# Four-way packed scores in a fused transformer pair: where the transposes of the first attention stand, and how the first half's finishing is cut

## The chip, the cores and the metric

The kernel runs on one core of one Trainium2 chip. The metric is device time in microseconds, the median of several executions. Profiles are of one execution of the program. TensorE is written PE, VectorE DVE, ScalarE ACT, GpSimd POOL and the DMA queue's engine SP.

## What is computed

Four layers on one sequence of T = 1024 tokens of D = 256 channels in fp32: an attention, a mixture of 8 experts, a gated linear attention, a mixture of 16 experts. Each is wrapped in two normalisations and a residual. Only the first matters here:

```
def _L0_attn_ref(X, ln_w, ln_b, W_in, W_out):
    Xn = (X - mu) * rsqrt(var + LN_EPS) * ln_w + ln_b
    Q, K, V = split(Xn @ W_in, 3)                # 16 heads of 16 channels
    Q, K = _rope(Q), _rope(K)
    probs = softmax(Q @ K.T / sqrt(16))          # every head: 1024 x 1024
    ctx = probs @ V
    return ctx @ W_out + X
...
x = L0_attn_X
x = x + _layernorm(_L0_attn_ref(_layernorm(x), ...))
x = x + _layernorm(_L0_ffn_ref(_layernorm(x), ...))
...
```

## The kernel before

`attention0` (L325) holds the first layer. The 16 heads lie in four groups of four, NG = 4; a head takes a slot of 32 rows (SLOT), so that a group of four fills the 128 rows of the array. The queries are taken in two halves of 512 tokens. That makes eight steps (query half, group), half 0 first.

The softmax is done in two passes over the scores. The generator `largest` (L380) computes for each step all products of queries and keys once, only for their maxima: it has 16 pulls per step, and each pull makes two products of 32 rows by 512 columns (L396), for two heads, and two maximum reductions on VectorE (L401). The negated maximum is put beside the query's channels. `attend` (L423) then computes the scores again, transposed (L443), with that maximum in them, exponentiates on ScalarE (L472) and multiplies with the values (`gather`, L437). It goes over TT = 8 tiles of keys, `st`, and in each over two pairs of heads. One pair is called a half-step here: two scores, two exponentials, and a gather of the tile before. In half-steps of st = 0 and in the first of st = 1 no gather is made. Sixteen half-steps make one attend.

The two passes are woven. `attend` yields between the two scores of a pair; there the outer loop calls `pull(1)`, which makes two products of `largest`, 20 pulls ahead of attend's own half-step from the ninth half-step on. Pair numbers run in opposite directions in the two generators, so the four products of a half-step use the four different strips of 32 rows of the array. The last 20 half-steps have no pull left; there `attend` goes another way (the branch `alone()`, L453), with four of its own scores together, exponentials at L461.

Three kinds of other work are put into the same place, between the first and the second score of a half-step, all by the order in which the generators emit:

- `turned` (L349): four transposes of 128 x 128 (L354) and a copy by ScalarE (L355). It brings keys (`kT`), queries for the first pass (`unsigned`, `qT`) and queries with their maximum (`signed`, `qTm`) into the layout of the products. `largest` calls it at its pulls s = 1, 9, 11, 13 and, at the very end, 15.
- what `beside` yields, in the first steps only: the projection of the later tokens, and `merged` (L245).
- from the fifth attend (n = NG) on, `finished(0)`, the finishing of the first half's 512 tokens: by token (transposes L492, reciprocal and product L497, L498), by channel (transposes L507, copy L509), `projected` (products with w_out L517, sum L524), and then `turn_over` (L191), which normalises, adds the residual, normalises again (`scales`: statistics L180 and L181, power on GpSimd L184, L185), writes `h` (L206) and leaves the transposes of `h` (L216, copy L217) on the list `todo`. One of these pieces is taken per half-step, so that all are made in the fifth attend.

The finishing of the second half goes onto `todo` after the last attend and is made among the experts' products.

PSUM tiles of this stage come from a pool of seven banks (`a_ps`, all under the tag b1), which scores of both passes and every transposed tile share; an eighth holds the gather's sum. A tile framework gives out these tiles, puts in the waits, and may move an instruction that is not ready behind others.

Of the kernel before, what the change touches and what calls it, by code (L numbers as in the profile page):

```python
# [15 lines left out]
P = 128  # L16
# [3 lines left out]
D = 256  # L20
# [29 lines left out]
class Net:  # L50
# [137 lines left out]
    def pair(self, v, tp):  # L188
        return [v[:, 2 * tp + i, :] for i in range(2)]

    def turn_over(self, ps, tts):  # L191

        nc = self.nc
        tp = tts[0] // 2
        xs = self.pair(self.x, tp)
        rs, nb = self.scales(self.pair(self.acc, tp))
        for i, x in enumerate(xs):
            nc.vector.scalar_tensor_tensor(  # L200
                x, self.acc[:, 2 * tp + i, :], rs[:, i : i + 1], x, ALU.mult, ALU.add
            )
        rs2, nb2 = self.scales(xs)
        h = self.row.tile([P, 2, D], F32, tag="h2", name="h")
        for i, x in enumerate(xs):
            nc.scalar.activation(  # L206
                h[:, i, :], x, AF.Identity, scale=rs2[:, i : i + 1], bias=nb2[:, i : i + 1]
            )
        for i, x in enumerate(xs):
            nc.gpsimd.tensor_scalar(x, x, nb[:, i : i + 1], None, ALU.add)  # L210

        def turned(ps):
            pt = ps.tile([P, KC, 2, P], F32, tag="b1", name="pt")
            for i in range(2):
                for k in range(KC):
                    nc.tensor.transpose(pt[:, k, i, :], h[:, i, k * P : (k + 1) * P], self.ident)  # L216
            nc.scalar.copy(  # L217
                self.hT[:, :, 2 * tp * P : (2 * tp + 2) * P], pt.rearrange("p k i t -> p k (i t)")
            )

        self.todo.extend([None, None, turned])

    def catch_up(self, ps, n):

# [100 lines left out]
    def attention0(self):  # L325
# [4 lines left out]
        with ExitStack() as ctx:  # L330
# [49 lines left out]
            def largest(first):  # L380
# [6 lines left out]
                for n, (qh, g) in enumerate(steps):  # L387
                    raw = raws.pop(n)
                    pm = self.small.tile([P, QT, G, 2], F32, tag="pm", bufs=2, name="pm")
                    for s, (kh, tt, pair) in enumerate(order):  # L390
                        if n == 0 and s == len(order) // 2:
                            turned(kT[:, 0, half(1)], 0, 1, 1)
                        scs = [ps.tile([P, HALF], F32, tag="b1", name="sc") for _ in range(2)]
                        for i, sc in enumerate(scs):
                            r = rows(2 * pair + i)
                            nc.tensor.matmul(  # L396
                                sc, raw[r, tt * P : (tt + 1) * P], kT[r, g, half(kh)],
                                start=True, stop=True,
                            )
                        for i, sc in enumerate(scs):  # L400
                            nc.vector.tensor_reduce(  # L401
                                pm[:, tt, 2 * pair + i, kh : kh + 1], sc, AX.X, ALU.max
                            )
                        if s % 2 == 1:
                            next(first, None)
                        if n > 0 and s == 1:
                            signed(n - 1)
                        if n + 1 < len(steps):
                            nqh, ng = steps[n + 1]
                            if nqh == 0 and s in (9, 11):  # L410
                                turned(kT[:, ng, half((s - 9) // 2)], ng, 1, (s - 9) // 2)
                            if s == 13:
                                unsigned(n + 1)
                        if s == len(order) - 1:
                            nc.vector.tensor_reduce(
                                qk[:, qh * QT : (qh + 1) * QT, 0, g * G : (g + 1) * G, DH : DH + 1],
                                pm, AX.X, ALU.max, negate=True,
                            )
                            if n == len(steps) - 1:
                                signed(n)  # L420
                        yield

            def attend(qh, g, alone):  # L423


                qm = ready.pop((qh, g))
# [23 lines left out]
                for st in range(TT):  # L450
                    pe = [pp.tile([P, 2, HALF], F32, tag="pe", name="pe") for _ in range(G // 2)]
                    pairs = list(reversed(range(G // 2)))
                    if alone():  # L453
# [8 lines left out]
                        if before is not None:  # L462
                            gather(st - 1, before, 1, True)
                        before = pe
                        yield
                        yield
                        continue
                    for at, pair in enumerate(pairs):
                        for i in range(2):
# [1 line left out]
                            score(sc, st, 2 * pair + i)  # L471
                            nc.scalar.activation(pe[pair][:, i, :], sc, AF.Exp, scale=scale)  # L472
                            if i == 0:
                                yield
                        if before is not None:
                            gather(st - 1, before, at)
                    before = pe
                gather(TT - 1, before, 1, True)
                nc.scalar.copy(oT[:, g, half(qh)], po)

            def finished(qh):

                tps = range(qh * QT // 2, (qh + 1) * QT // 2)
                cxs = {}

                def by_token(tp, i, ps):
                    if i == 0:
                        cxs[tp] = self.row.tile([P, 2, H, DH], F32, tag="h2", name="cx")
                    tt = 2 * tp + i
                    pt = ps.tile([P, H, SLOT], F32, tag="b1", name="pt")  # L490
                    for g in range(NG):
                        nc.tensor.transpose(  # L492
                            pt[:, g * G : (g + 1) * G, :].rearrange("p h c -> p (h c)"),
                            oT[:, g, tt * P : (tt + 1) * P], self.ident,
                        )
                    rec = self.small.tile([P, H, 1], F32, tag="rec", name="rec")
                    nc.vector.reciprocal(rec, pt[:, :, DH : DH + 1])  # L497
                    nc.vector.tensor_tensor(  # L498
                        cxs[tp][:, i, :, :], pt[:, :, 0:DH], rec.to_broadcast([P, H, DH]), ALU.mult
                    )  # L500

                def by_channel(tp, ps):
                    cx = cxs[tp].rearrange("p i h c -> p i (h c)")
                    pc = ps.tile([P, KC, 2, P], F32, tag="b1", name="pc")
                    for i in range(2):
                        for k in range(KC):
                            nc.tensor.transpose(pc[:, k, i, :], cx[:, i, k * P : (k + 1) * P], self.ident)  # L507
                    cT = self.row.tile([P, KC, 2, P], F32, tag="cT", bufs=2, name="cT")
                    nc.scalar.copy(cT, pc)  # L509
                    cxs[tp] = cT  # L510

                def projected(tp, ps):
                    cT = cxs.pop(tp)
                    po = ps.tile([P, 2, D], F32, tag="b1", name="po")
                    for i in range(2):
                        for k in range(KC):
                            nc.tensor.matmul(  # L517
                                po[:, i, :], cT[:, k, i, :], self.w_out[:, k, :],
                                start=(k == 0), stop=(k == KC - 1),
                            )  # L520

                    for i in range(2):
                        tt = 2 * tp + i
                        nc.vector.scalar_tensor_tensor(  # L524
                            self.acc[:, tt, :], self.x[:, tt, :], self.rs0[:, tt : tt + 1],
                            po[:, i, :], ALU.mult, ALU.add,
                        )
                    self.turn_over(ps, [2 * tp, 2 * tp + 1])

                for tp in tps:  # L530
                    for i in range(2):
                        yield lambda ps, tp=tp, i=i: by_token(tp, i, ps)
                for tp in tps:
                    yield lambda ps, tp=tp: by_channel(tp, ps)
                for tp in tps:
                    yield lambda ps, tp=tp: projected(tp, ps)

            first, rsx = self.normed0((0, 1))
            self.load_first(rsx[:, 0:1])
# [13 lines left out]
                nc.gpsimd.tensor_tensor(self.rs0, ve, self.nhalf, ALU.pow)  # L553
                yield from self.merged(ps)

            left = [2 * TT * len(steps)]
            ahead = largest(beside())

            def pull(n):
                for _ in range(n):  # L560
                    if left[0]:
                        next(ahead)
                        left[0] -= 1

            pull(2 * TT + 2)
            after = iter(())
            for n, (qh, g) in enumerate(steps):
                if n == NG:
                    after = finished(0)
                for i, _ in enumerate(attend(qh, g, lambda: left[0] == 0)):  # L570
                    pull(3 if n == 0 and i == 7 else 1)
                    step = next(after, None)
                    if step is not None:
                        step(ps)
                    else:
                        self.catch_up(ps, 1)
            for step in after:
                step(ps)
            self.catch_up(ps, len(self.todo))
            self.todo.extend(finished(1))  # L580


# [737 lines left out]
```

## Time and profile before

| | |
|---|---|
| median of 3 timed runs | 1323.51 us (1322.59 to 1324.91) |
| profiled execution | 1320.31 us, its span 1318.5 us |
| mean granted TensorE clock | 0.986 |
| busy: PE, DVE, ACT, POOL | 1244.9, 731.6, 497.4, 149.4 us |
| attends of the first attention, from the first gather at 76.5 us to the last copy at 339.0 us | 262.5 us |

In rows of the profile L with a number is a line of the kernel, `sc<-qTm,kT` the tiles written and read, and "32*128 32x512" a product with 32 active rows and 128 active columns and 512 columns streamed. A product in fp32 shows as two matmul records. What stands in brackets or behind the last bar is the idle time of that engine before the instruction and who ended it. The starts are in microseconds from the first instruction; ends of matmuls are modelled.

### The profile page before, as it was taken

What the parts mean: (1) busy time and instruction counts of PE and PEld (TensorE: products, weight loads), DVE (VectorE), ACT (ScalarE), POOL (GpSimd) and SP (SyncE); (2) the same over time, 40 slices, a digit from 0 to 9 for tenths busy, and PEclk for the clock granted to TensorE, in tenths of its full rate; (3) what the DMA queues carried; (4) which work ended last, traced back from release to release, by engine and by line L of the source; (5) the groups of instructions that cost most, each with busy time, mean ns of one, the idle gap of its engine ahead of it and who ended that gap; (6) DMA issues with size and microseconds to landing.
All of it is one profiled execution on the core that took longest, in us unless ns stands there. A gap on an engine that the chain in (4) does not pass through costs nothing. (4 is left out here: it accounts for less than half of the span.)

```text
span 1318.5 us, 15710 instructions
## 1 busy us (share of the span) xinstructions
PE 1244.9 (94%) x6088; PEld 729.0 (55%) x6088; DVE 731.6 (55%) x1657; ACT 497.4 (38%) x911; POOL 149.4 (11%) x137
## 2 busy tenths in 40 slices
PE   5899999999999998889999999999998799999997
PEld 2433333332456565456676767676767456655655
DVE  4675665563243335777586777777775633233334
ACT  3256663566441111454545444445445122011111
POOL 2100000100010002111212121211112400000000
PEclk9999999899999999899999999999999899999999
DMA  6000000000005101200212112130211103723000
GB/s 189 1 1 1 1 1 1 0 1 1 1 1 172 53 12 53 83 33 32 72 33 72 50 56 72 33 103 33 73 32 34 61 1 95 218 80 108 32 25 32
DMA packets 38923, 64.42 MB, mean 49 GB/s; under 512 B 4776, under 2 KB 28552, under 8 KB 38848
## 3 DMA queue, kind: packets, MB, share of 16 engines
q1 hardware_dynamic: 38848, 63.41, 15.2%
q8 instruction: 48, 0.79, 0.3%
q14 instruction: 27, 0.22, 0.1%
HBM read 62.12 MB, written 1.28 MB: 48 GB/s over the span
## 5 line engine op out<-in xcount | busy, mean ns | idle before, releaser
L401 DVE TENSOR_REDUCE pm<-sc 128x1 f32<-128x512 f32 x256 | 163.4, 684 | 94.2 <-PE sc L443 56.5
L443 PE MATMUL sc<-qTm,kT 32*128 32x512 f32 x512 | 170.5, 644 | 2.4 <-DVE pm L401 1.7
L648 DVE TENSOR_TENSOR mid<-sg,pu 128x512 f32<-128x512 f32 (+1 forms) x82 | 56.4, 687 | 200.3 <-PE pu L645 166.7
L472 ACT ACTIVATE pe<-sc 128x512 f32<-128x512 f32 x216 | 119.1, 595 | 87.5 <-PE sc L443 59.3
L647 ACT ACTIVATE sg<-pg 128x512 f32<-128x512 f32 (+1 forms) x82 | 48.9, 596 | 270.2 <-PE pg L645 270.0
L396 PE MATMUL sc<-kT,qT 32*128 32x512 f32 x512 | 140.1, 643 | 1.7 <-ACT qT L355 1.1
L969 ACT ACTIVATE sn<-pt,shift,rs 128x128 f32<-128x128 f32 x256 | 93.6, 470 | 106.9 <-DVE shift L965 106.8
L929 PE MATMUL px<-hT,w_l1a 128*128 128x512 f32 x256 | 124.1, 597 | 4.1 <-issue 3.5
L921 DVE SCALAR_TENSOR_TENSOR y<-px,cp,y 128x1023 f32<-128x1023 f32 (+5 forms) x102 | 123.2, 1211 | 2.5 <-ACT y L915 2.5
L184 POOL TENSOR_TENSOR rs<-ve,nhalf 128x2 f32<-128x2 f32 (+1 forms) x29 | 20.8, 717 | 702.6 <-DVE ve L183 698.1
L645 PE MATMUL pg<-hT,w_l1f 128*128 128x512 f32 (+1 forms) x200 | 96.0, 603 | 0.7 <-ACT hT L217 0.7
L671 DVE TENSOR_TENSOR acc<-acc,po 128x512 f32<-128x512 f32 (+1 forms) x61 | 41.1, 674 | 99.7 <-PE po L663 99.7
L645 PE MATMUL pu<-hT,w_l1f 128*128 128x512 f32 (+1 forms) x200 | 94.6, 595 | 0.0
L663 PE MATMUL po<-w_l1f,mid 128*128 128x256 f32 (+1 forms) x400 | 87.5, 379 | 0.0
L443 PEld LDWEIGHTS sc<-qTm,kT 32*128 32x128 f32 x512 | 52.5, 185 | 63.2 <-issue 42.0
L964 POOL TENSOR_TENSOR rs<-ve,nhalf 128x8 f32<-128x8 f32 x32 | 52.4, 1638 | 299.5 <-DVE ve L963 244.7
L437 PE MATMUL po<-pe,va 128*32 128x256 f32 (+1 forms) x832 | 83.3, 444 | 1.9 <-ACT pe L461 1.2
L663 PEld LDWEIGHTS po<-w_l1f,mid 128*128 128x128 f32 (+1 forms) x400 | 76.0, 190 | 13.4 <-issue 3.3
L1063 PE MATMUL pg<-hT,w_l1a 128*128 128x512 f32 x128 | 61.9, 609 | 6.5 <-DVE og L1145 4.8
L645 PEld LDWEIGHTS pu<-hT,w_l1f 128*128 128x128 f32 (+1 forms) x200 | 38.2, 191 | 48.9 <-issue 48.7
L437 PEld LDWEIGHTS po<-pe,va 128*32 128x32 f32 x832 | 18.3, 108 | 84.6 <-issue 63.7
L645 PEld LDWEIGHTS pg<-hT,w_l1f 128*128 128x128 f32 (+1 forms) x200 | 37.9, 192 | 44.7 <-issue 43.3
(196 smaller groups left out, 1936.1 us busy)
## 6 DMA issues: line engine op xcount, KB each, us to landing
spread<-rows SPq DMA_DIRECT2D x32, 512.0 KB, 4.5
w<-w SPq DMA_DIRECT2D x16, 512.0 KB, 5.0
w_l1f<-in_e_gT SPq DMA_DIRECT2D x4, 640.0 KB, 4.0
w_l1f<-in_e_uT SPq DMA_DIRECT2D x4, 640.0 KB, 5.3
w_l1f<-in_e_dT SPq DMA_DIRECT2D x4, 640.0 KB, 7.2
w_l0f<-in_e_wg SPq DMA_DIRECT2D x4, 512.0 KB, 3.7
w_l0f<-in_e_wu SPq DMA_DIRECT2D x4, 512.0 KB, 5.8
w_l0f<-in_e_wd SPq DMA_DIRECT2D x4, 512.0 KB, 6.7
```

What stands on the lines that cost most here:

```text
L396: nc.tensor.matmul(sc, raw[r, tt * P : (tt + 1) * P], kT[r, g, half(kh)], start=True, stop=True,)
L401: nc.vector.tensor_reduce(pm[:, tt, 2 * pair + i, kh : kh + 1], sc, AX.X, ALU.max)
L437: nc.tensor.matmul(po[rows(j), c], va[:, st, g * G + j, :], pe[j // 2][:, j % 2, c], start=(st == 0), stop=(st == TT - 1 and quarter == 1),)
L443: nc.tensor.matmul(sc, kT[rows(j), g, st * P : (st + 1) * P], qm[rows(j), :], start=True, stop=True,)
L472: nc.scalar.activation(pe[pair][:, i, :], sc, AF.Exp, scale=scale)
L645: nc.tensor.matmul(p, w(k), self.hT[:, k, c], start=(k == 0), stop=(k == KC - 1))
L648: nc.vector.tensor_tensor(mid, sg, pu, ALU.mult)
L663: nc.tensor.matmul(po[:, i, :], left[:, at * P : (at + 1) * P], right, start=(n == 0), stop=(n == len(pieces) - 1),)
L921: nc.vector.scalar_tensor_tensor(y[:, at:hi], px[:, at - j : hi - j], column(cw + 4 * h + 3 - j), y[:, at:hi], ALU.mult, ALU.add,)
L929: nc.tensor.matmul(px[:, c], w[:, k, hh * DK : (hh + 1) * DK], self.hT[:, k, c], start=(k == 0), stop=(k == KC - 1),)
L969: nc.scalar.activation(sn[:, n, :], pts[n // 4][:, n % 4, :], AF.Identity, scale=rs[:, n : n + 1], bias=shift[:, n : n + 1],)
L1063: nc.tensor.matmul(pg, wg[:, k, hh * DK : (hh + 1) * DK], self.hT[:, k, c], start=(k == 0), stop=(k == KC - 1),)
```

## The change

It has two parts. First, what `largest` turns is no longer emitted inside a pull: the pull returns it as a function (`then`), and the outer loop calls it when `attend` has emitted its second score, the exponentials and the gather of the half-step. The pulls ahead of the first attend are 20 where they were 18, there each `then` is called at once, and the half-step that had three pulls (n = 0, i = 7) has one.

Second, the finishing of the first half is a generator of its own, `finished_slowly`, with a copy of `turn_over` that yields between its pieces. It is advanced once at the end of every half-step, behind the gather and behind `then`, and yields twice after each piece; so a piece comes every second half-step, and the whole takes 62 of the 64 half-steps of the last four attends. Its projection takes one token tile at a time, with a PSUM tile of its own. `finished(1)` does what it did. The diff, cut to its core:

```
+    def turn_over_slowly(self, ps, tp, acc):
...
+        mv = small("mv", 2)
+        for i in range(2):
+            acc(i)
+            yield
+            stats(mv, i, accs[i])
+            yield
+        rs, nb = scale(mv)
+        yield
+        mv = small("mv", 2)
+        for i, x in enumerate(xs):
+            nc.vector.scalar_tensor_tensor(x, accs[i], rs[:, i : i + 1], x, ALU.mult, ALU.add)
+            yield
+            stats(mv, i, x)
+            yield
+        rs2, nb2 = scale(mv)
+        h = self.row.tile([P, 2, D], F32, tag="h2", name="h")
+        for i, x in enumerate(xs):
+            nc.scalar.activation(
+                h[:, i, :], x, AF.Identity, scale=rs2[:, i : i + 1], bias=nb2[:, i : i + 1]
+            )
+            yield
+        for i, x in enumerate(xs):
+            nc.gpsimd.tensor_scalar(x, x, nb[:, i : i + 1], None, ALU.add)
+        self.turn(ps, h, tp)
+        yield
...
                         if s % 2 == 1:
                             next(first, None)
+                        then = None
                         if n > 0 and s == 1:
-                            signed(n - 1)
+                            then = lambda n=n: signed(n - 1)
                         if n + 1 < len(steps):
                             nqh, ng = steps[n + 1]
                             if nqh == 0 and s in (9, 11):
-                                turned(kT[:, ng, half((s - 9) // 2)], ng, 1, (s - 9) // 2)
+                                then = lambda ng=ng, kh=(s - 9) // 2: turned(kT[:, ng, half(kh)], ng, 1, kh)
                             if s == 13:
-                                unsigned(n + 1)
+                                then = lambda n=n: unsigned(n + 1)
...
                             if n == len(steps) - 1:
-                                signed(n)
-                        yield
+                                then = lambda n=n: signed(n)
+                        yield then
...
                             if i == 0:
-                                yield
+                                yield True
                         if before is not None:
                             gather(st - 1, before, at)
+                        yield False
...
+            def finished_slowly():
+
+                yield
+                yield
+                for tp in range(QT // 2):
+                    cx = self.row.tile([P, 2, H, DH], F32, tag="h2", name="cx")
+                    for i in range(2):
+                        tt = 2 * tp + i
+                        by_token(tt, cx[:, i, :, :], ps)
+                        yield
+                        yield
+                    cT = by_channel(cx, ps)
+                    yield
+                    yield
+
+                    def acc(i):
+                        po = ps.tile([P, D], F32, tag="b1", name="po")
+                        projected(2 * tp + i, cT[:, :, i, :], po)
+
+                    for _ in self.turn_over_slowly(ps, tp, acc):
+                        yield
+                        yield
...
-            pull(2 * TT + 2)
+            while pulled < 2 * TT + 4:
+                then = pull()
+                if then:
+                    then()
             after = iter(())
             for n, (qh, g) in enumerate(steps):
                 if n == NG:
-                    after = finished(0)
-                for i, _ in enumerate(attend(qh, g, lambda: left[0] == 0)):
-                    pull(3 if n == 0 and i == 7 else 1)
-                    step = next(after, None)
-                    if step is not None:
-                        step(ps)
-                    else:
-                        self.catch_up(ps, 1)
-            for step in after:
-                step(ps)
-            self.catch_up(ps, len(self.todo))
+                    after = finished_slowly()
+                then = None
+                for inside in attend(qh, g, lambda: pulled == count):
+                    if inside:
+                        then = pull()
+                        continue
+                    if then:
+                        then()
+                        then = None
+                    next(after, None)
+            for _ in after:
+                pass
```

## The prediction

> **What bounds the kernel now.** I read the page first, then a table of windows cut at the eight calls of `attend` (ends at 138.17, 169.58, 201.00, 256.54, 288.02), then the timeline of TensorE inside one of them, then all engines around 201 to 256.
>
> ```profile
> L401 DVE TENSOR_REDUCE pm<-sc 128x1 f32<-128x512 f32 x256 | 163.4, 684 | 94.2 <-PE sc L443 56.5
> L443 PE MATMUL sc<-qTm,kT 32*128 32x512 f32 x512 | 170.5, 644 | 2.4 <-DVE pm L401 1.7
> L396 PE MATMUL sc<-kT,qT 32*128 32x512 f32 x512 | 140.1, 643 | 1.7 <-ACT qT L355 1.1
> ```
>
> ```profile
> 103.90:138.17 34.27, 34.27 (x258) 11.96 (x257) 20.62 (x34) 20.70 (x38) 0.00 (x0) 1.00 0.00 1
> 169.58:201.00 31.42, 31.42 (x249) 10.97 (x248) 20.62 (x34) 19.31 (x36) 0.00 (x0) 1.00 0.01 1
> 201.00:256.54 55.54, 53.25 (x297) 19.60 (x296) 30.77 (x74) 23.64 (x44) 6.47 (x8) 0.91 0.00 1
> 256.54:288.02 31.48, 31.48 (x249) 10.96 (x249) 20.67 (x34) 19.37 (x36) 0.00 (x0) 1.00 0.01 1
> 317.50:336.80 19.30, 18.80 (x128) 4.74 (x128) 0.00 (x0) 16.94 (x34) 0.00 (x0) 1.00 0.00 1
> ```
>
> The columns of a window are its length, busy PE, PEld, DVE, ACT, POOL, the granted clock and the DMA share. In every attend TensorE has no idle time, VectorE and ScalarE are busy two thirds of it: TensorE's order sets the time. 31.42 holds two turns (`turned`), 34.27 four, so **one turn costs (34.27-31.42)/2 = 1.43 us** and an attend without turns 28.57. 55.54 holds two turns and the whole finishing of the first half, so **the finishing costs 55.54-31.48 = 24.06 us**. In the last row, where the first pass has run out, TensorE (97%) and ScalarE (88%) are both nearly full and VectorE idle.
>
> ```profile
> 149.87 0.69 PE L443 MATMUL sc<-qTm,kT 32*128 32x512 f32 x1
> 149.88 0.70 PE L396 MATMUL sc<-kT,qT 32*128 32x512 f32 x2
> 150.94 0.64 PE L437 MATMUL po<-pe,va 128*32 128x256 f32 x8
> 151.51 0.69 PE L443 MATMUL sc<-qTm,kT 32*128 32x512 f32 x1
> ...
> 155.00 0.69 PE L443 MATMUL sc<-qTm,kT 32*128 32x512 f32 x1
> 156.06 0.66 PE L354 MATMUL pt<-ident,qk 128*128 128x128 f32 x4
> 156.65 1.12 PE L443 MATMUL sc<-qTm,kT 32*128 32x512 f32 x2
> 157.70 0.64 PE L437 MATMUL po<-pe,va 128*32 128x256 f32 x8
> 158.27 0.69 PE L443 MATMUL sc<-qTm,kT 32*128 32x512 f32 x1
> ```
>
> Start, duration, line. A plain half-step: four products (each two passes) lie in four different 32-row strips and run side by side, 149.87 to 150.94 = 1.07 us for all; the gather takes 0.57; the step is 1.64 (others 1.85, mean 1.75). A half-step with a turn: three products 1.06, transposes 0.59, then the fourth product **alone** from 156.65 to 157.70, again 1.05, gather 0.57: 3.27. The fourth product is paid twice because the transposes stand before it.
>
> **The turns.** Behind the gather a turn costs its own transposes, 0.59, or less where the step was one of 1.85. Saved per turn: 1.43-0.55 = 0.9 (bounds 0.5 and 1.05). Turns inside half-steps: 4 in attend 1 (0 is the first), 2 each in 2, 3, 4 and 5: 12 x 0.9 = 10.8 us. ScalarE's copy of a turn (0.59) follows its two exponentials (1.09), 1.68 in a half-step that now lasts 2.2, so it hides. The last turn (attend 6) waits at 311.12 for the final maximum; from 308.34 to 314.61 two steps take 6.27 where 1.64+2.16+0.59 = 4.4 would do: 1.8 saved. In attend 0 two turns save 1.8; the half-step with three pulls (5.06 us, two turns) becomes two ordinary ones of 2.3, against 5.06+1.75 now, 2.1 saved; but the two pulls put ahead of the attends fall where VectorE is full (2 x 1.29 = 2.6 lost). They fill TensorE's 0.67 us wait for the copy at 69.53: together +1.8. **Turns: 14.4 us.**
>
> [...]
>
> **The finishing.** It leaves the quartets too, and is spread as 30 pieces over every second half-step of attends 4 to 7: 21 while the first pass still runs, 9 in the last stretch. Pieces stand two half-steps (3.5 us) apart, so transposes and projections find their inputs ready. Cost then, from rows of 201 to 256:
> - TensorE, always on the path: transposes of 4 tokens' contexts, 2 by channel, 1 turn, 7 x 0.59 = 4.1; projections (1.92 us for two tokens at 221.80) 4 x 0.96 = 3.8. Sum 8.0; the second turn lies in the last stretch, below.
> - VectorE: per token 0.67 (reciprocal 0.25, product 0.42), sum 0.43, statistics 0.5 twice, update 0.43; per pair two `scale` of 1.2. All on 0.45 us slack per half-step (1.75-1.29), 0.9 per piece; a `scale` of 1.2 makes the next reductions 0.8 late and seven PSUM banks hold that. Not hidden in the first four half-steps of an attend, which have no gather and where VectorE is full (eight reductions in 4.99 us): one `scale` and one update, 1.6, and 0.3 for three context pieces. Sum 1.9.
> - ScalarE: in attend 5 the first `h` waits for the `scale` before it, with the next exponentials behind it in the queue and the fourth product behind those: 0.7 (bounds 0 and 1.8).
> - The last stretch: `h` twice 0.55 and the hT copy 0.59 on a full ScalarE, transposes 0.5 on a full TensorE beside them: 1.6. Everything of VectorE there is free.
> - GpSimd: four powers (0.71) and four adds (0.93 each) move later in its queue, which was busy 6.47 of 55 us, and nobody waits for the adds in attention. SP issues no DMA in any moved step.
>
> ```profile
> 226.61 0.16 DVE L185 SCALAR_TENSOR_TENSOR nb<-mv,rs 128x2 f32<-128x2 f32 x1 [0.82 <-POOL rs L184]
> 236.22 1.12 PE L443 MATMUL sc<-qTm,kT 32*128 32x512 f32 x2 [1.69 <-DVE pm L401]
> 236.00:244.00 8.00, 7.78 (x22) 2.66 (x22) 3.65 (x9) 3.62 (x7) 2.53 (x3) 0.60 0.00 0
> 244.00:252.00 8.00, 8.00 (x55) 2.59 (x54) 3.59 (x7) 3.63 (x7) 0.00 (x0) 0.76 0.00 0
> ```
>
> Sum 8.0+1.9+0.7+1.6 = 12.2, so **24.06-12.2 = 11.9 saved**. Part of the 24 is the clock: after VectorE's burst (it waits 0.82 for GpSimd, TensorE then waits 1.69 for VectorE) the granted clock is 0.60 and 0.76, worth 8 x 0.40 + 8 x 0.24 = 5.1 us. [...] 103.90 to 138.17 has four turns and a clock of 1.00. I let the dip go with the stalls; if it comes elsewhere the sum is 5.1 less.
>
> **Sum.** 14.4+11.9 = 26.3. The profiled execution took 1320.3 (span 1318.5), which gives 1294.0; the median of the timed runs, 1323.5, lies 3.2 above it, so I predict 1297. What follows attention (experts) reads hT of the first half, now written two rounds of keys (some 4 us) before attention ends; nothing is expected to wait there (bound 2 us).
>
> **Rivals.**
> - The order is not what the code says (10%). The framework may move an instruction: at 309.40 the gather stands ahead of transposes that the code emits first. If turns slip back into the quartets, only the finishing gains: 1323.5-11.9 = 1312. Against: every other turn of before lies where the code puts it.
> - The finishing stays dear (12%): its pieces hold the queues one by one, or the clock dips all the same; half of its gain and some of the turns' go: about 1308.
> - Better than the sum (8%): inserted groups give ScalarE time, 1.85 steps become 1.64, attention meets no stall: 1287.
> - Slower (5%): PSUM. A step now opens a fifth tile in seven banks and holds it into the next step, whose fourth product must then wait and run alone, 1.05 us. With 12 finishing groups and 17 turns that is 29 x 1.05 = 30.5, more than the 26.3 gained: 1327.7. It decides from 25 split quartets on. For it: steps of 1.85 show that the fourth product already starts late at times (waiting for an exponential). Against: after 2.2 us the previous step's exponentials and first maxima have ended, which leaves four banks.
>
> **Numbers.** Main case 65%: 1290 to 1304. With the costs' bounds (turns 10 to 18, finishing saving 6 to 16) and the neighbours, 8 in 10 lies in 1288 to 1310. Runs of this kernel spread over 0.17%, so about 0.2% (2.6 us) can be told from no change; faster 0.93, slower 0.05, and 0.02 for the dear finishing at its worst, which ends near no change.
>
> **What would show it.** In the after profile: no L396 or L443 product alone between transposes and a gather; attends 2 and 3 near 29.7 us, attend 1 near 30.8; clock 1.00 through attends 4 and 5, which take about 34 and 33; no 1.69 us wait of scores on `pm`. Wrong if attends 2 and 3 stay at 31.4 (turns not moved or a lone product remains), if half-steps after a turn show lone fourth products, or if the last stretch grows by over 4 us.

## The result, and the profile after

The changed kernel took 1309.08 us (median of four executions, 1308.1 to 1309.54) where the kernel before took 1324.21 (1322.59 to 1326.6): a ratio of 0.9883 [0.9866, 0.99], or 15.1 us. Its profiled execution took 1309.17 (span 1307.4). Measured a second time, in five rounds beside other kernels (after_again below), the same program took 1301.4 (ratio 0.9829 [0.9783, 0.9874], span of its profile 1298.9). Whether both measurements used the same chip is not on record. The two profiles of the one program differ by 8.5 us: 5.2 of these lie before the end of attend 0, 0.9 in attends 4 to 7 and 2.4 behind attention. So its gain is known only as 15 to 22 us.

Cut at the end of each attend (the copy of its sum), in us from the profiles:

| | to the end of attend 0 | attends 1, 2, 3 | attends 4, 5, 6, 7 | what follows | span |
|---|---|---|---|---|---|
| before | 106.62 | 34.26 31.42 31.42 | 55.60 31.42 28.91 19.36 | 979.5 | 1318.5 |
| after, first | 110.30 | 30.92 29.75 29.74 | 38.14 31.27 35.05 19.95 | 982.3 | 1307.4 |
| after, second | 105.11 | 30.92 29.75 29.75 | 37.28 30.88 35.37 19.95 | 979.9 | 1298.9 |

Summed up against the forecast:

| us saved | forecast | first | second |
|---|---|---|---|
| attends 1 to 3 (8 turns) | 8 x 0.9 = 7.2 | 6.7 | 6.7 |
| attends 4 to 7 (4 turns, the last turn, the finishing) | 3.6 + 1.8 + 11.9 = 17.3 | 10.9 | 11.8 |
| to the end of attend 0 | 1.8 | -3.7 | 1.5 |
| what follows | 0 | -2.8 | -0.4 |
| sum | 26.3 | 11.1 | 19.6 |

"What follows" takes between 977.6 and 983.6 us in the profiles of the other changed kernels below, whose work there is the same. So the 2.8 us of the first column lie within what differs from one execution to the next.

The costliest groups of the page of the changed kernel, and its windows at the calls of attend (1, 3, 4, 5, and the last stretch; columns as in the prediction):

```profile
L449 DVE TENSOR_REDUCE pm<-sc 128x1 f32<-128x512 f32 x256 | 163.0, 685 | 81.6 <-PE sc L493 49.4
L493 PE MATMUL sc<-qTm,kT 32*128 32x512 f32 x512 | 152.9, 643 | 2.3 <-ACT pe L522 1.6
L444 PE MATMUL sc<-kT,qT 32*128 32x512 f32 x512 | 139.5, 670 | 1.7 <-ACT qT L403 1.1
```

```profile
107.58:138.49 30.91, 30.91 (x257) 11.64 (x256) 20.62 (x34) 20.26 (x38) 0.00 (x0) 1.00 0.01 1
168.24:197.98 29.74, 29.74 (x249) 10.80 (x248) 20.61 (x34) 19.09 (x36) 0.00 (x0) 1.00 0.01 1
197.98:235.40 37.42, 35.68 (x269) 12.67 (x268) 27.40 (x55) 20.95 (x39) 3.26 (x4) 0.98 0.00 1
235.40:267.19 31.79, 31.79 (x253) 11.75 (x253) 19.33 (x31) 19.19 (x35) 0.00 (x0) 0.92 0.00 1
303.00:322.90 19.90, 19.21 (x132) 5.05 (x132) 0.00 (x0) 17.43 (x35) 0.00 (x0) 1.00 0.00 1
```

The scores of attend (L493) are the same 512 records with nearly the same mean (643 ns for 644), but cover 152.9 us where they covered 170.5: fewer of them run with nobody beside them. Attends 1 and 3 lose 3.35 and 1.68 with VectorE's and ScalarE's work unchanged. In the third row the forecast fails to come: TensorE is idle for 37.42 - 35.68 = 1.74 us, and the row after it has a clock of 0.92.

What a turn looks like now, in TensorE's timeline (start, duration, line):

```profile
156.60 0.64 PE L487 MATMUL po<-pe,va 128*32 128x256 f32 x8
157.18 0.66 PE L402 MATMUL pt<-ident,qk 128*128 128x128 f32 x4
157.76 0.69 PE L493 MATMUL sc<-qTm,kT 32*128 32x512 f32 x1
157.77 0.70 PE L444 MATMUL sc<-kT,qT 32*128 32x512 f32 x2
...
158.83 0.64 PE L487 MATMUL po<-pe,va 128*32 128x256 f32 x8
```

From gather to gather 2.23 us, where it was 3.27: the transposes stand alone (0.58), and all four products follow together in 1.07. No lone product is left here.

What went wrong in attend 4 stands in its timeline with all engines; in brackets is the idle time before, and who ended it:

```profile
227.92 0.16 DVE L208 SCALAR_TENSOR_TENSOR nb<-mv,rs 128x2 f32<-128x2 f32 x1 [0.82 <-POOL rs L207]
228.00 0.48 DVE L221 SCALAR_TENSOR_TENSOR x<-acc,rs,x 128x256 f32<-128x256 f32 x1
...
230.00 0.45 DVE L221 SCALAR_TENSOR_TENSOR x<-acc,rs,x 128x256 f32<-128x256 f32 x1
...
232.15 0.16 DVE L208 SCALAR_TENSOR_TENSOR nb<-mv,rs 128x2 f32<-128x2 f32 x1 [0.81 <-POOL rs L207]
232.23 2.48 DVE L449 TENSOR_REDUCE pm<-sc 128x1 f32<-128x512 f32 x4
232.35 0.60 ACT L228 ACTIVATE h<-x,nb,rs 128x256 f32<-128x256 f32 x1 [3.81 <-DVE nb L208]
...
233.48 1.99 PE L493 MATMUL sc<-qTm,kT 32*128 32x512 f32 x2 [1.60 <-ACT pe L522]
```

The code spreads the first `nb`, the two updates of x, the second `nb` and `h` over some ten half-steps, about 18 us. On the chip they lie within 4.5. Twice VectorE waits 0.8 for GpSimd with reductions ready behind, then it owes four of them in a row (2.48). ScalarE, with `h` at the head of its queue, does nothing for 3.81, its exponential comes late, and the fourth product runs alone after a wait of 1.60. In the kernel before, TensorE waited 1.69 at this place for a maximum; here it waits for an exponential, and behind both stands a burst on VectorE. The same happens to the second pair in attend 6, where the last turn then waits 2.15 for its maximum:

```profile
296.21 0.66 PE L402 MATMUL pt<-ident,qk 128*128 128x128 f32 x4 [2.15 <-DVE qk L464]
```

VectorE's own timeline shows the order. In the change (first three lines) `ve`, the first step of `scale`, stands right behind the statistics of the second sum, and `nb` is next. In pinned, an experiment below with the same instructions, four reductions stand between the statistics and `ve`, four behind `nb`, and then comes the update of x, as the code emits them:

```profile
226.25 0.43 DVE L201 BATCH_NORM_STATS2 st<-acc 128x6 f32<-128x256 f32 x1
226.71 0.18 DVE L202 BATCH_NORM_AGGREGATE mv<-st 128x2 f32<-128x6 f32 x1
226.93 0.17 DVE L206 TENSOR_SCALAR ve<-mv 128x2 f32<-128x2 f32 x1
```

```profile
224.38 0.42 DVE L201 BATCH_NORM_STATS2 st<-acc 128x6 f32<-128x256 f32 x1
224.83 0.18 DVE L202 BATCH_NORM_AGGREGATE mv<-st 128x2 f32<-128x6 f32 x1
224.93 1.25 DVE L449 TENSOR_REDUCE pm<-sc 128x1 f32<-128x512 f32 x2
228.09 1.29 DVE L449 TENSOR_REDUCE pm<-sc 128x1 f32<-128x512 f32 x2 [1.91 <-PE sc L493]
229.30 0.16 DVE L206 TENSOR_SCALAR ve<-mv 128x2 f32<-128x2 f32 x1
230.28 0.16 DVE L208 SCALAR_TENSOR_TENSOR nb<-mv,rs 128x2 f32<-128x2 f32 x1 [0.82 <-POOL rs L207]
230.36 2.48 DVE L449 TENSOR_REDUCE pm<-sc 128x1 f32<-128x512 f32 x4
232.75 0.47 DVE L221 SCALAR_TENSOR_TENSOR x<-acc,rs,x 128x256 f32<-128x256 f32 x1
```

The framework has pulled the normalisation of the pair forward to its second sum. One wait of 0.82 with four reductions behind it stands in pinned too, and TensorE then waits only 0.24 (at 231.10). So a single wait of this kind costs little; what stops the products seems to be two of them in one burst, with `h` in front of the exponentials.

### The profile page after: what moved, and what is told of

It reads as the page before. It is cut to its first block, busy times and chain, and to the rows that moved or that the text cites. A ratio compares the mean times of both kernels' runs of the same rounds, so it can differ in the third digit from the quotient of the medians.

```text
span 1307.4 us, 15704 instructions
## 1 busy us (share of the span) xinstructions
PE 1230.2 (94%) x6088; PEld 727.1 (56%) x6088; DVE 732.5 (56%) x1657; ACT 495.6 (38%) x911; POOL 149.1 (11%) x137
## 3 DMA queue, kind: packets, MB, share of 16 engines
q1 hardware_dynamic: 38848, 63.41, 15.1%
## 5 line engine op out<-in xcount | busy, mean ns | idle before, releaser
L493 PE MATMUL sc<-qTm,kT 32*128 32x512 f32 x512 | 152.9, 643 | 2.3 <-ACT pe L522 1.6
L493 PEld LDWEIGHTS sc<-qTm,kT 32*128 32x128 f32 x512 | 50.8, 184 | 55.8 <-issue 32.3
L184 POOL TENSOR_TENSOR rs<-ve,nhalf 128x2 f32<-128x2 f32 (+1 forms) x25 | 17.5, 701 | 472.7 <-DVE ve L183 468.2
```

The lines of the kernel that those rows point to most:

```text
L493: nc.tensor.matmul(sc, kT[rows(j), g, st * P : (st + 1) * P], qm[rows(j), :], start=True, stop=True,)
```

## The experiments

Each kernel was timed in five rounds beside the kernel before on the same chip; the first four shared one chip, the next four another, the last two a third. The medians of before were 1323.6, 1323.73 and 1322.54. In all of them "behind" means behind the gather.

**turns_only**: the turns as in the change; the finishing in large pieces among the products, as before but for one order (see burst_behind); the pulls of before.

```
-            while pulled < 2 * TT + 4:
+            while pulled < 2 * TT + 2:
...
-                    after = finished_slowly()
+                    after = finished(0)
...
                     if inside:
-                        then = pull()
+                        thens = [pull() for _ in range(3 if n == 0 and i == 7 else 1)]
...
+                        finish()
                         continue
```

> The changed placement of the turns alone: the finishing stands among the products as before, and the first pass keeps its old pulls (18 ahead, three in one half-step). Theory (the turns bring most of the gain, the finishing little, because its VectorE chain is still made in one burst): attends 1, 2 and 3 as in the changed kernel (30.9, 29.7, 29.7 us), attend 4 about 53.8, in all 12 to 14 us below before. Rival (the gain is shared about evenly, as predicted, and something at the start ate part of it): the same 12 to 14, but then the changed kernel's further gain must show in attend 4 to 7 and its loss at the start. Against both: if under 8 us, the placement of the turns is not what moved attends 1 to 3.

1314.44 (1311.37 to 1316.96), 0.9927 [0.9903, 0.995]. Attends 1 to 7: 30.92, 29.75, 29.75, 55.88, 29.74, 28.34, 19.37. Attends 1, 2 and 3 give their turns exactly as in the change, and attend 5 gives its two. Attend 4 gives nothing (55.60 before), where 1.8 was expected. In the kernel before, one of its two turns stood in the half-step of the 1.69 wait, and the other (251.04) beside the transposes of `h`, which leave the fourth product alone with or without the turn. The kernel also has a new wait of 1.38 there, for the reason given under burst_behind, so what the two turns are worth in attend 4 is not shown by it. In all this half alone brings about 9, not the 12 to 14 expected.

**finish_only**: the finishing as in the change; the turns among the products, the pulls of before.

```
-                            then = lambda n=n: signed(n - 1)
+                            signed(n - 1)
...
-                        then = pull()
+                        for _ in range(3 if n == 0 and i == 7 else 1):
+                            pull()
```

> The small pieces of the finishing alone, over four attends behind the gather; the turns stand among the products as before, and the first pass keeps its old pulls. Theory: attends 1 to 3 as before (34.3, 31.4, 31.4 us), attend 4 about 39, attends 5 to 7 about 9 us longer than before, in all 4 to 7 us below before. Rival (the prediction's own sum): 11.9 us below before.

1316.88 (1308.39 to 1324.89), 0.9947 [0.9926, 0.9969]. Attends 4 to 7 take 38.34, 32.53, 36.13, 19.95, together 8.3 less than before; attends 1 to 3 are those of before. With turns_only (2.0 less in attends 4 to 7) that is 10.3 of the 10.9 of the change: the parts add up within 0.6.

**burst_behind**: the turns as in the change; the finishing in its large pieces of before, one per half-step, but behind.

```
-                    after = finished_slowly()
+                    after = finished(0)
...
-                    next(after, None)
+                    step = next(after, None)
+                    if step is not None:
+                        step(ps)
+                    else:
+                        self.catch_up(ps, 1)
```

> The changed kernel, but the first half's finishing in its old eight large pieces, one per half-step in attend 4, all behind the gather. Theory (what counts is that the pieces leave the quartets of products; the small pieces do not stay spread anyway): attend 4 takes about 41 us, attends 5 to 7 lose what the spread pieces cost them (about 7 us less than in the changed kernel), so within 3 us of the changed kernel. Rival (spreading is what helps): attend 4 stays near 50 us and the kernel is 6 us or more above the changed one.

1302.87 (1302.11 to 1309.93), 0.9851 [0.9826, 0.9877]. Attends 4 to 7: 46.71, 29.75, 28.06, 19.37, in sum 123.89; the change's are 124.41 and 123.48. Attend 4 was dearer than expected, but leaving the quartets alone brings the finishing all that the change gets from it. The spreading, as the framework carries it out, brought nothing beyond that. In the timeline the old stall is still there, as in the change (second line):

```profile
216.84 2.08 PE L578 MATMUL po<-w_out,cT 128*128 128x256 f32 x4 [1.26 <-DVE acc L582]
226.20 1.20 PE L493 MATMUL sc<-qTm,kT 32*128 32x512 f32 x2 [1.66 <-DVE pm L449]
```

The first line is a wait that the kernel before does not have. The changed code's `finished` emits each token's sum right behind that token's products (`projected`), where before the products of both tokens came first; both use one PSUM tile, and the second token's products wait for the first one's sum. So the large pieces are not quite those of before, and `finished(1)` too has this new order. In "what follows" no cost of it can be seen.

**pinned**: the change, with each piece tied in the issue order: nothing of it on VectorE may go ahead of the last reduction emitted, nothing on ScalarE ahead of the last exponential. No instruction is added or left out.

```
-                            nc.vector.tensor_reduce(
+                            self.red = nc.vector.tensor_reduce(
...
-                            nc.scalar.activation(pe[pair][:, i, :], sc, AF.Exp, scale=scale)
+                            self.exp = nc.scalar.activation(pe[pair][:, i, :], sc, AF.Exp, scale=scale)
...
-                    next(after, None)
+                    with self.tc.issue_after(self.red.ins), self.tc.issue_after(self.exp.ins):
+                        next(after, None)
```

> The changed kernel with the issue order held: each small piece's VectorE instructions stand behind the last reductions emitted before them, its ScalarE instructions behind the last exponential, so that the normalisation is really spread. Theory (the framework pulled the VectorE chain forward into one burst, and that cost attend 4 about 4 us and attend 6 about 3): attend 4 near 33 us, no wait of scores of over 1 us on maxima or exponentials there, clock 1.00 in attend 5; 5 to 8 us below the changed kernel. Rival (VectorE and ScalarE work cannot hide in this stretch, however it is spread): within 2 us of the changed kernel, the waits being many and small.

1295.5 (1295.08 to 1297.98), 0.9788 [0.9767, 0.9808]. Attends 4 to 7: 32.78, 31.97, 31.74, 20.31, in sum 116.80, 7.6 less than the change. Its windows over attends 4 and 5 and the last stretch:

```profile
194.20:224.83 30.63, 30.63 (x253) 11.59 (x253) 22.30 (x41) 18.58 (x35) 0.00 (x0) 1.00 0.01 1
224.83:256.65 31.82, 31.50 (x253) 10.75 (x252) 22.43 (x44) 20.62 (x38) 3.26 (x4) 1.00 0.00 1
289.00:309.50 20.50, 19.66 (x133) 5.28 (x134) 0.00 (x0) 18.33 (x38) 1.85 (x2) 1.00 0.00 1
```

TensorE has no gap in attend 4 and 0.32 in attend 5, the clock is 1.00 in both, and VectorE's work is level (22.30 and 22.43) where the change had 27.40 and 19.33. This is the finishing as the prediction had it. In the whole, the interval of pinned lies clear of the change's first one and overlaps that of its second (after_again); the attends tell the two kernels apart, the second total does not.

**after_again**: the changed kernel once more.

> The changed kernel once more, on the chip of this call. Theory (about 6 us of its time in the first profile were a half-speed clock from 53 to 70 us that comes by chance, since kernels with the same instructions up to there had none): runs of two kinds, some near 1302 to 1303 with a mean clock near 0.985, some near 1308 to 1309 with 0.978 to 0.982. Rival (the dip belongs to the changed kernel): all runs within 1 us of 1309.

1301.4 (1299.44 to 1310.56). Its six executions are 1299.44, 1299.46, 1300.71, 1302.09, 1302.12 and 1310.56, with mean clocks of 0.989, 0.989, 0.987, 0.987, 0.985 and 0.976: within this measurement time follows the clock, (1310.56 - 1299.45)/13 = 0.9 us for each 0.001. The four of the first measurement have 0.978 to 0.984. That accounts for the larger part of the distance and not for all of it: 1308.1 at 0.984 is some 4 us longer than the relation gives, and this rest is open.

**old_pulls**: the change with the pulls of before, 18 ahead and three in half-step 7 of attend 0, all their turns behind.

```
-            while pulled < 2 * TT + 4:
+            while pulled < 2 * TT + 2:
...
-                        then = pull()
+                        thens = [pull() for _ in range(3 if n == 0 and i == 7 else 1)]
```

> The changed kernel with the old pulls: 18 ahead of the first attend, three in its eighth half-step, whose turns all stand behind the gather. Theory (the new pull schedule gained about 2 us, by the end of attend 0: 104.5 in profiles without an early clock dip, 106.6 before): end of attend 0 at 105.4, as in the kernel with only the turns moved, less its share of an early dip; 0 to 2 us slower than the changed kernel. Rival (the two pulls ahead cost what they save): no slower, or faster by up to 1 us.

1302.02 (1300.34 to 1310.63), 0.9838 [0.9796, 0.988], like after_again. The new schedule of pulls is worth nothing that can be seen in the whole. The first product of attend 0 shows why, here in old_pulls and in after_again, neither of which has a half-clock stretch between the start-up and it:

```profile
67.59 0.69 PE L493 MATMUL sc<-qTm,kT 32*128 32x512 f32 x1 [0.68 <-ACT qTm L403]
70.20 0.69 PE L493 MATMUL sc<-qTm,kT 32*128 32x512 f32 x1
```

From there attend 0 takes 35.06 (67.59 to 102.65) with the old pulls and 34.91 with the new ones. Of the latter 1.7 are a half-clock stretch of 3.4 at 76; in the first profile of the change, which has none in attend 0, it takes 32.97. So the schedule takes some 2 us out of attend 0 and puts 2.6 ahead of it. Attend 0 itself takes 37.09 in the kernel before, so its turns save the other 2.03.

**pin_dve**: pinned, but only VectorE's part tied (`self.red`), ScalarE's left free.

```
-                    with self.tc.issue_after(self.red.ins), self.tc.issue_after(self.exp.ins):
+                    with self.tc.issue_after(self.red.ins):
```

> As the kernel with the order held, but only VectorE's instructions are held, ScalarE's not. Theory (VectorE's burst made the loss; ScalarE's h follows by data): within 1 us of the kernel with both held (1295.5), attend 4 near 32.8 us. Rival (the exponentials queued behind h made the loss): 2 us or more slower than 1295.5, attends 5 and 6 longer by as much.

1301.57 (1295.98 to 1310.38), 0.9822 [0.9777, 0.9868]. Attends 4 to 7: 32.78, 32.45, 33.97, 19.95. Attend 4 is whole with VectorE tied alone. Attend 6 is 2.2 longer than in pinned; its timeline says why:

```profile
288.79 0.60 ACT L228 ACTIVATE h<-x,nb,rs 128x256 f32<-128x256 f32 x1 [1.33 <-DVE nb L208]
...
289.93 2.03 PE L487 MATMUL po<-pe,va 128*32 128x512 f32 x8 [1.50 <-ACT pe L511]
```

Where the first pass has run out no reduction comes any more that could hold the pieces back, `h` goes ahead of the exponentials, and the gather waits for them. So both queues have to be held: VectorE for the first pair, ScalarE for the last. The median lies 6 us above the 1295.5 that was expected, with runs from 1296 to 1310. The total cannot tell this kernel from the change or from pinned (the intervals overlap); the attends can.

**pinned_vec**: pinned, and the rotation of the last two token tiles on VectorE in place of GpSimd.

```
-                    self.project0(tt, xn, ps, qk, va, nc.vector if tt < 6 else nc.gpsimd)
+                    self.project0(tt, xn, ps, qk, va, nc.vector)
```

> The kernel with the order held, and the rotation of the last two token tiles on VectorE where GpSimd did it. Theory (the early clock dip follows TensorE's idle 1.6 and 0.7 us at 52 to 55 us, which end with GpSimd's rotation): that idle time goes, 1 to 2 us gained before attend 0, and no dip between 50 and 70 in any run, so runs within 2 us of each other near 1293.5. Rival (VectorE is full in this stretch and its reductions get late): 1 us slower or more than 1295.5, idle time on reductions in its place.

**pinned_vec2**: the same kernel again.

> The kernel with the order held and the rotation on VectorE once more, beside the one with h later on the same chip: near 1293.5 us, attends 4 to 7 as in its first profile (32.8, 32.0, 31.7, 20.3 us); runs above 1296 have a lower mean clock, by 0.001 for every 1.1 us or so.

1293.54 (1291.31 to 1299.49), 0.9766 [0.9727, 0.9804], and 1290.17 (1290.12 to 1294.37), 0.9764 [0.9747, 0.9782]. Attend 0 ends at 103.26 and 101.51, the difference a dip of 3.4 us. The wait at the end of the projections shrinks from 1.59 in the kernel before to

```profile
52.61 0.33 PE L402 MATMUL pt<-ident,qk 128*128 128x128 f32 x1 [0.60 <-POOL qk L371]
```

and the clock is 1.00 from 50 to 70 us in the profile of pinned_vec, where the first profile of the change had a dip (a stretch of half clock) of 17.1 us. With the longer wait the clock from 50 to 60 was 0.63 in the change, 0.66 in turns_only and 0.66 in finish_only, but 1.00 in before, burst_behind and pinned; so few do not show that the shorter wait prevents the dip. Other dips still come, and the runs of pinned_vec lie 8 us apart where 2 were expected. In time it is about 1 us in the profile and no difference from pinned that the intervals can tell.

**h_later**: pinned_vec, with a yield moved: `h` comes a piece after the `scale` that it needs, not in the same piece.

```
             nc.vector.scalar_tensor_tensor(x, accs[i], rs[:, i : i + 1], x, ALU.mult, ALU.add)
-            yield
+            if i == 1:
+                yield
             stats(mv, i, x)
...
         rs2, nb2 = scale(mv)
+        yield
         h = self.row.tile([P, 2, D], F32, tag="h2", name="h")
```

> The kernel with the order held and the rotation on VectorE, and h one piece later than the scale it needs (the first update and the statistics behind it share a piece in return). Theory (in attend 5 h waited 1.26 us for nb, the exponentials behind it came late, and the fourth product of one half-step ran alone, 2.83 us for 1.75): that half-step becomes ordinary, attend 5 near 30.9 us for 31.97, the run 1 us below the kernel with h at once. Rival (h costs its own place in ScalarE's queue): no change in attend 5.

1293.14 (1290.75 to 1294.52), 0.9777 [0.9762, 0.9793]. It is the one stall that pinned still had in attend 5. There (first two lines, pinned) ScalarE stands still for 1.26 and the step takes 2.83; with the yield (third line, h_later) `h` waits for nothing, and the step takes 1.75:

```profile
248.37 0.60 ACT L228 ACTIVATE h<-x,nb,rs 128x256 f32<-128x256 f32 x1 [1.26 <-DVE nb L208]
249.51 1.12 PE L493 MATMUL sc<-qTm,kT 32*128 32x512 f32 x2
```

```profile
247.71 0.60 ACT L230 ACTIVATE h<-x,nb,rs 128x256 f32<-128x256 f32 x1
```

Attend 5 falls from 31.97 to 30.98. This 1.0 us is clear in the attend and lost in the whole: on the same chip pinned_vec2 took 1290.17, and the ranges of the two overlap.

## Why the prediction came out as it did

**The bound** was right where it was used: TensorE's order sets the time of attends 1 to 3 within 0.01 us in every kernel with the turns behind. "In every attend TensorE has no idle time" is too much; the prediction's own row of attend 4 has 55.54 - 53.25 = 2.29.

**The turns**: right. Each saves (34.26 - 30.92)/4 = 0.84 for 0.9. The forecast had taken 0.55 for the transposes; they cost 0.58. The lone product carries it, 1.05 us in the prediction's rows: attends 1 to 3, where none is left, saved 6.7. Attend 5 saves its two in turns_only (1.68), attend 6 only 0.57 there and 0.85 in burst_behind, of 1.8: the final maximum still has to be waited for (0.85 us in both).

**The finishing**: the step that failed is "is spread as 30 pieces over every second half-step". It was costed at 12.2 and took (124.41 - 106.93) = 17.5 in the first profile and 16.5 in the second, where 106.93 is what attends 4 to 7 take without any finishing (29.75 + 29.75 + 28.06 + 19.37, from burst_behind and turns_only). Attend 4 is taken here to be like attend 5 without it. In each of the two profiles some 3.4 of this are the clock: 6.8 us at half speed. The costs in the sum were enough for pieces that stay where the code puts them: pinned, with the same instructions and no half-clock stretch, took 116.80 - 106.93 = 9.9, so the 12.2 was 2.3 too high. The prediction named the framework's moving of instructions as a rival, but for the turns only; they stayed. What it moved was VectorE's small instructions, which no one needed early. Why it thought VectorE free for them was not looked into.

**ScalarE**: "in attend 5 the first `h` waits for the `scale` before it" was right as a mechanism, and pinned shows it: 0.7 expected, 1.0 measured by h_later. In the change it sits in attend 4 and is 3.81 long.

**The last stretch**: 1.6 expected, 0.6 in the change (19.95 against 19.36), part of whose work had been pulled into attend 6, and 0.9 in pinned.

**The pulls**: right, step by step. The turns of attend 0 saved 2.03 for 1.8; the half-step with three pulls saved some 2 for 2.1; the two pulls ahead cost 2.6 as forecast, with the 0.67 wait for the copy gone. The prediction's terms make 2.0, not 1.8. In it the schedule comes to next to nothing, and so it does in old_pulls; the 2 us were an expectation of that run alone.

**The clock**: "I let the dip go with the stalls" holds in pinned (1.00 in attends 4 and 5) and not in the change, whose stalls stayed. And the first stretch brought a dip that no step of the forecast moved. That the row with four turns had a clock of 1.00 says little: four turns are 4 x 0.59 = 2.4 of 34 us, too few to show what transposes do to the clock.

**The signs** that it named: attends 1 to 3 came as said, and no turn in them left a product alone. Attends 4 and 5 took 38.14 and 31.27 for 34 and 33, at clocks of 0.98 and 0.92 for 1.00. Scores no longer waited 1.69 on `pm` but 1.60 on `pe`.

**Rivals.** "The finishing stays dear" gave 1308 by pieces that hold the queues and a clock that dips all the same. The first measurement, 1309.08, reads as if it were this case whole. By the table it is so in part: 6.4 of the 15.2 us missing in that profile lie in attends 4 to 7, 5.5 in the first stretch and 2.8 behind attention. In the second the 6.4 are 5.5, hardly more than 1 us is missing elsewhere, and 1301.4 lies in the main case's 1290 to 1304, where 1309.08 lies outside it and just inside the wider range. "Slower" by PSUM did not come: attends 1 to 3 have no lone fourth product. "Better than the sum" did not come for the change; pinned_vec2 reached 1290.17 by an edit that was not part of it.

A part of the agreement is luck: the burst and the clock loss, which were not forecast, were in part made up for by costs that were put 2.3 too high.

**What stays open**: whether the change is worth 15 or 22 us in a given run. 5.2 of the 8.5 us between its two profiles lie before the end of attend 0, where the first had 17.1 us at half clock and the second 3.4; what sets such stretches off is not shown.

## What to carry to other kernels

Where four small products share the array, put everything else between groups and none of it inside; the four transposes of a turn inside cost a whole product's time again (1.05 us). When work is cut fine to lie under another engine's slack, look at each engine's queue in the order as built, because a scheduler may gather it into one burst again; tie the pieces to the work that they are to follow, on every queue where somebody waits. A gain of under 1% of a kernel whose clock moves is told by the stretch that it changes, with the clock beside it, and only then by the total.

## What the runs showed of the hardware

The granted clock fell to 0.50 for stretches of 3.4, 6.8 and 10.2 us in the profile of before and of 3.4, 6.8, 10.2 and 17.1 us in the first profile of the change, multiples of 3.41 but for the one at the end of each profile. Here in windows of the latter:

```profile
235.00:240.00 5.00, 5.00 (x27) 1.55 (x29) 0.00 (x0) 1.18 (x2) 0.00 (x0) 0.50 0.01 3
55.00:60.00 5.00, 5.00 (x18) 2.33 (x17) 3.08 (x5) 0.59 (x1) 0.00 (x0) 0.50 0.00 0
```

The last number but two is the clock. The first row follows the waits in attend 4 shown above, TensorE's 1.60 among them. The second is part of 17.1 us from 53 on, in the profile whose attend 0 ended at 110.30; the second profile of the same program had one of 3.4 us at 76 and ended it at 105.11.

Waits of the same length were followed by a half clock in one profile and not in another. In before TensorE waited 1.69 until 236.22, and the clock was 0.50 from 237.7 to 247.9; in the first profile of the change it waited 1.60 until 233.48, and the clock was 0.50 from 233.6 to 240.4. At the last turn's wait (2.15 in the first profile of the change), TensorE was idle for 3.41 - 1.48 = 1.93 us of a window in the second profile, and the next window is at half clock (first two lines). In the first profile 1.08 and 1.17 are idle in two windows, and both are at full clock (last two lines), as is what follows from 296 to 320:

```profile
287.85:291.26 3.41, 1.48 (x12) 0.73 (x12) 2.59 (x9) 0.00 (x0) 0.68 (x1) 1.00 0.00 0
291.26:294.67 3.41, 3.41 (x18) 0.90 (x14) 0.16 (x1) 3.16 (x7) 1.87 (x3) 0.50 0.00 0
```

```profile
291.63:295.04 3.41, 2.33 (x18) 0.29 (x10) 2.46 (x9) 1.09 (x2) 0.73 (x1) 1.00 0.00 0
295.04:298.45 3.41, 2.24 (x18) 0.88 (x18) 1.99 (x8) 0.51 (x1) 0.70 (x1) 1.00 0.00 0
```

The waits at 50 us likewise: before has one of 1.59 until 53.62 and one of 0.68 until 54.62, the first profile of the change has 1.59 until 51.91 and 0.68 until 52.91. The clock was 1.00 from 50 to 70 in before, and 0.50 from 52.7 to 69.8 in the change. What decides between the two is not shown. Nor is what sets off the dips behind attention: the one at 363 us in the first profile of the change comes where TensorE's timeline marks no wait after 325. Measured twice, one program's medians stood 7.7 us apart, about half of what this change brought in the first of them.
